# A message-passing layer on one core: the work after the last group of edges, in another order and another form

## The chip, the cores and the metric

The kernel runs on one core of one Trainium2 chip. The metric is device time in microseconds (us); the time before is the median of three runs, 1493.0 us (1492.52 to 1494.01). Durations of single instructions come from one separate execution that the hardware profiler recorded; that execution is longer as a whole (see the section on the profile).

## The reference

There are N = 6250 nodes with F = 64 features, and E = 200000 edges sorted by destination. For every edge a small network makes M = 9 weights, the source node's row is multiplied with them and with `W_tp`, and the messages are summed by destination node. The sums are scaled and shifted per node, added to `x` and normalised:

```python
w = silu(edge_attr @ W1 + b1) @ W2 + b2
h_src = features[src]
msg = einsum('ef,em,fmg->eg', h_src, edge_sh * w, W_tp)
agg = segment_sum(msg, dst, num_segments=N) / sqrt(16)
gamma, beta = split(silu(c_noise[:, None] @ Wn1 + bn1) @ Wn2 + bn2, 2, axis=-1)
x = layernorm(x + agg * (1 + gamma) + beta, axis=-1)
```

## The kernel before

**Tiles and groups.** The edges are cut into tiles of 128 and the tiles into 98 groups of 16 (`NBLK`, `KB`); group 97, the last, has only 11 tiles. The nodes are cut into 49 blocks of 128 (`NJ`). Since the edges are sorted, the edges of one tile end in at most W = 7 neighbouring nodes, and a group's edges in at most 256 nodes.

**What happens to a group.** Most of its source rows are gathered into `hs` by indirect DMAs that GpSimd issues six groups ahead. The last four tiles' rows (three in every fifth group) are instead picked from a copy of `x` in SBUF by matmuls: `pick(g, t)` (L488) multiplies one-hot matrices with `x` in 14 fp32r matmuls (L500) into the PSUM tile `px`, and VectorE reduces that to `hs` in two instructions (L509, L511). `hidden` (L429), `second` (L447) and `weights` (L457 to L467) make the edge weights, spread over the 7 windows, in `a`. `windows(g)` (L533) multiplies each tile's `hs` with its `a` into `pz`, and ScalarE copies `pz` into the SBUF tile `ztw` (L543), a slot for each of four groups. In the last group, tiles of even and odd number go to two PSUM tiles (the second is `pz__`).

**From windows to nodes.** `project(q)` multiplies the `ztw` of a pair of groups (2q-1 and 2q) with `W_tp` (L579), copies the result to SBUF (L582), turns it with a transpose (L585) and splits it into two fp32r halves, high and low, in `r` (L553 on ScalarE, L554 on VectorE). A group without a partner, as the last, is multiplied the other way round, without the transpose (L573). `marks(q)` (L563) makes the one-hot matrices `c` that say to which of 256 nodes a window belongs. `place(q)` (L595) multiplies `r` with `c`: features (high and low half) on partitions, 256 nodes on columns. The first 128 columns, added to the carried columns of the pair before, are `yt` of a finished block (L604); the other 128 are kept as `carry` (L601). `bring` (L612) multiplies `yt` with an identity and so puts the nodes on partitions and sums the two halves; `finish` runs the instructions of `finish_nodes` (L716 to L731), among them one square root on ScalarE (L728), and puts the store of the output (L382) on a list; SyncE issues it later.

**The order** is written out by hand: each engine gets its instructions in program order. In the loop each group's steps are put between the matmuls of the picks of the next group, so that TensorE always has pick matmuls to do. The end of the kernel, after the loop, is a list of calls. Before the change it is: `second(97)`, picks 1 and 2 of group 97, `windows(96)`, pick 3 of group 97 (the last pick), `project(48)`, which is the pair of groups 95 and 96, the three last tiles of `windows(97)`, transpose, halves and `place(48)`, `bring` of blocks 46 and 47 and most of their `finish`, the eight first tiles of `windows(97)`, the rest of that `finish`, `project(49)` (group 97 alone), `place(49)`, `bring` of block 48, its `finish`, and the stores. After them every engine reads a flag that decides on a general path (not taken here), and the program ends.

```python
            pick(g, 3)
            marks(g // 2)
            turn = project(g // 2)
            windows(g, [ZT])
            ends = []
            for f in turn + place(g // 2, psum.tile([P, 2 * P], F32, tag="s", name="ps_l")):
                f()
```

Of the kernel before, what the change touches and what calls it, by code (L numbers as in the profile page):

```python
# [7 lines left out]
F32 = mybir.dt.float32  # L8
# [59 lines left out]
def gnn_resnorm_kernel(ctx: ExitStack, tc: tile.TileContext, x, src, dst, dst_row, ea, sh, cn,  # L68
# [18 lines left out]
    with ExitStack() as fast:  # L87
# [354 lines left out]
        def second(g):  # L442

            s = st.pop(g)
            p2[g] = psum.tile([P, 2, 2 * P], F32, tag="s", name=f"p2_{g}")
            for c in range(KB // 4):
                nc.tensor.matmul(p2[g][c * D:(c + 1) * D, 0, :].rearrange("p (i e) -> p i e", i=2), w2p,  # L447
                                 s[:, :, c * P:(c + 1) * P], start=True, stop=True)
            p2s[g] = work.tile([P, 2 * P], F32, tag="p2s", name=f"p2s{g}")
            nc.scalar.activation(p2s[g], p2[g][:, 0, :], AF.Identity, bias=b2c)  # L450
# [37 lines left out]
        def pick(g, t, other=()):  # L488


            other = [f for fs in other for f in fs]
            q = picked(g) if g < NBLK else 0
            if t >= q:
                for f in other:
                    f()
                return
            px = psum.tile([P, F, J], F32, tag="px", name=f"px{g}_{t}", bufs=2)
            for h in range(J):
                for i in range(2):
                    nc.tensor.matmul(px.rearrange("p f l -> p (f l)"), hot_k[g, t][:, h, :],  # L500
                                     xs[i][:, h].rearrange("p f l -> p (f l)"),
                                     start=(h == 0 and i == 0), stop=(h == J - 1 and i == 1))
                    if i == 1 and other:
                        other.pop(0)()
            for f in other:
                f()
            xm = late.tile([P, F, J], F32, tag="xm", name=f"xm{g}_{t}")
            c = (g + 1) * Q - q + t
            nc.vector.scalar_tensor_tensor(xm, li[:, None, :].to_broadcast([P, F, J]), jl[:, c:c + 1], px,  # L509
                                           op0=ALU.is_equal, op1=ALU.mult)  # L510
            nc.vector.tensor_reduce(hs[g][:, tiles(g) - q + t, :], xm, AX.X, ALU.add)  # L511
# [7 lines left out]
        def windows(g, k0s=None):  # L519

            nk = tiles(g)
            end = g == NBLK - 1
            hsg, ag = hs[g], a[g]
            z = zs[g] if g in zs else sums(g)


            for k0 in range(0, nk, ZT) if k0s is None else k0s:
                n = min(ZT, nk - k0)
                pz = [psum.tile([P, ZT // 2, M, W], F32, tag="pz", name=f"pz{g}_{k0}", bufs=2)]
                pz.append(psum.tile([P, ZT // 2, M, W], F32, tag="px", name=f"pz{g}_{k0}_", bufs=2) if end else pz[0])  # L530
                for k in range(n):
                    v = k % 2
                    mm = nc.tensor.matmul(pz[v][v * F:(v + 1) * F, k // 2].rearrange("p m w -> p (m w)"),  # L533
                                          hsg[:, k0 + k, :], ag[:, k0 + k].rearrange("p m w -> p (m w)"),
                                          start=True, stop=True)
                    if k0 + k == 0:

                        for d in hs_dma.pop(g)[(g not in SPG):]:
                            tc.add_manual_dep(mm.ins, d.ins.name, mybir.DependencyInfo(
                                mybir.DependencyClass.Sync, mybir.DependencyReason.DATA), reason="rows of the group")  # L540
                for v in range(2):
                    for h in range(2):
                        nc.scalar.copy(  # L543
                            z[h * F:(h + 1) * F, 0:5 - h, k0 + v:k0 + n:2, :].rearrange("p m k w -> p k m w"),
                            pz[v][v * F:(v + 1) * F, 0:(n + 1 - v) // 2, h:M:2, :])

# [10 lines left out]
        def marks(q):  # L557

            for g in pair(q):
                if g in hot:  # L560
                    continue
                hot[g] = work.tile([KW, 2 * P], F32R, tag="c", name=f"c{g}")
                nc.vector.tensor_scalar(hot[g], nf[0:KW], nid[0:KW, g:g + 1], None, op0=ALU.is_equal)  # L563
# [26 lines left out]
        def place(q, pd):  # L590

            gs = pair(q)

            def part(k):
                nc.tensor.matmul(pd, r[q][:, k].rearrange("p s f -> p (s f)"), hot.pop(gs[k]),  # L595
                                 start=(k == 0), stop=(k == len(gs) - 1))
                if k == len(gs) - 1:
                    r.pop(q)
                    if q < NJ:
                        carry[q] = work.tile([P, P], F32, tag="carry", name=f"carry{q}")  # L600
                        nc.scalar.copy(carry[q], pd[:, P:2 * P])  # L601
                    if q > 0:
                        yt[q - 1] = work.tile([P, P], F32, tag="yt", name=f"yt{q}", bufs=3)
                        nc.vector.tensor_add(yt[q - 1], pd[:, 0:P], carry.pop(q - 1))  # L604

            return [lambda k=k: part(k) for k in range(len(gs))]

        def bring(j0, j1, py, ends=None):


            def part(j):
                nc.tensor.matmul(py[:, j - j0], yt.pop(j), ident2, start=True, stop=True)  # L612
                if j == j1 - 1:
                    finish(j0, j1, py[:, 0:j1 - j0], ends)

            return [lambda j=j: part(j) for j in range(j0, j1)]
# [21 lines left out]
        with tc.manual_schedule(), tc.tile_pool(name="temp", bufs=1) as temp:  # L638
            setup(temp)

            for i in range(NBLK):
                if i + AHEAD < NBLK:
                    gather(i + AHEAD)
                while stores:
                    stores.pop(0)()
                if i % LB == 0 and i + LB < NBLK:
                    if i > 0:
                        load(i + LB)
                    near(i + LB)
                if i % LB == 1 and i + 1 + LB < NBLK:  # L650
                    load_keys(i + 1 + LB)
                if i % 4 == 3 and i + 1 < NJ:
                    gate_load(i + 1)
                for g in SPG:
                    if AHEAD - SPS < g - i <= AHEAD:
                        load_rows(g, (AHEAD - g + i) * SPR)
                more = []
                if i + 2 < NBLK:
                    keys(i + 2)
                    more = [lambda: hots(i + 2, 0, 2)]  # L660
                pick(i + 1, 0, [nodes(i), more])
                if i + 2 < NBLK:
                    hots(i + 2, 2, Q)
                if 56 <= i <= 58:
                    reach(i - 56)
                if i + 2 < NBLK:
                    hidden(i + 2)
                if i == NBLK - 2:
                    break
                second(i + 1)  # L670
                windows(i)
                turn = project(i // 2) if i % 2 == 1 else []
                if i % 4 == 1 and i - 1 < NJ:
                    gate_hidden(i - 1)
                pick(i + 1, 1, [weights(i + 1), turn])
                for t in range(2, Q):
                    pick(i + 1, t)

            g = NBLK - 1
            second(g)  # L680
            nc.scalar.activation(root, eps, AF.Sqrt)
            pick(g, 1, [weights(g)])
            pick(g, 2)
            sums(g)
            windows(g - 1)
            pick(g, 3)
            marks(g // 2)
            turn = project(g // 2)
            windows(g, [ZT])
            ends = []  # L690
            for f in turn + place(g // 2, psum.tile([P, 2 * P], F32, tag="s", name="ps_l")):
                f()
            marks(NBLK // 2)
            for f in bring(NJ - 3, NJ - 1, psum.tile([P, FB, F], F32, tag="s", name="py_l"), ends):
                f()
            windows(g, [0])
            ends.pop()()
            project(NBLK // 2)
            ps = psum.tile([P, 2 * P], F32, tag="p1", name="ps_n")
            for f in place(NBLK // 2, ps) + bring(NJ - 1, NJ, psum.tile([P, 1, F], F32, tag="r", name="py_n")):  # L700
                f()
            while stores:
                stores.pop(0)()

# [205 lines left out]
```

## Time and profile before

| what | value |
|---|---|
| median of three runs | 1493.0 us |
| the profiled execution | 2388.12 us, of which the span from first to last instruction is 2386.3 us |
| granted TensorE clock, mean | 0.841 of full speed |
| TensorE matmul busy | 1675.3 us (70%) |
| VectorE, ScalarE, GpSimd busy | 1206.6, 521.1, 1109.7 us |
| pick matmuls (L500) | 5208, of 406 ns each on average |
| GpSimd idle before its gathers, waiting for L533 | 825.8 us |
| VectorE's last instruction (L731) | ends 2380.40 us after the span's start |

The profiled execution takes 1.6 times as long as an ordinary one, so the shares of the page describe a stretched body. Its end can be read by itself: it is a short stretch, every instruction of it has a start and a duration, and the pick matmuls there take 3.02 us for 14, about 0.21 us each. Each view below counts microseconds from the start of the span.

### The profile page before, as it was taken

How to read it: one execution, taken by the hardware profiler on the slowest of the kernel's cores; microseconds unless marked ns; L12 is line 12 of the kernel's file. 1: busy time of each engine (PE TensorE's matmuls, PEld its weight loads, DVE VectorE, ACT ScalarE, POOL GpSimd, SP SyncE). 2: the span in 40 equal slices, each digit the busy share in tenths (PEclk: the TensorE clock that was granted, in tenths of full speed). 3: DMA queues.
4: the chain of work that ended last, by engine and by line, in shares of the span. 5: the costliest groups of instructions: out<-in, count | busy, mean ns of one | idle time of the engine just before them, and what ended most of it. 6: DMA issues, size and time to landing. Idle time of an engine off the chain costs nothing. (4 is left out here: it accounts for less than half of the span.)

```text
span 2386.3 us, 34188 instructions
## 1 busy us (share of the span) xinstructions
PE 1675.3 (70%) x10858; PEld 1367.1 (57%) x10858; DVE 1206.6 (51%) x2157; ACT 521.1 (22%) x1326; POOL 1109.7 (47%) x1177
## 2 busy tenths in 40 slices
PE   3076777676776767677767677677777676877797
PEld 2065656564655655556656556565656564656586
DVE  3154545454545454545555545454545454545476
ACT  1021212121212121211222222121212121212133
POOL 7644444444444545444545454545444544444410
PEclk7598888888888988887888898788887888888898
DMA  3121111111111111111111111111111111111110
GB/s 114 34 62 40 47 34 41 36 46 37 38 35 42 41 39 38 44 37 38 35 36 44 38 37 45 35 36 35 47 34 37 36 45 35 37 35 46 33 38 5
DMA packets 90264, 96.13 MB, mean 40 GB/s; under 512 B 36744, under 2 KB 51290, under 8 KB 90074
## 3 DMA queue, kind: packets, MB, share of 16 engines
q1 hardware_dynamic: 52122, 53.89, 7.9%
q0 software_dynamic: 37376, 38.35, 7.1%
q8 instruction: 89, 1.46, 0.2%
q10 hardware_dynamic: 576, 1.61, 0.2%
q14 instruction: 101, 0.83, 0.1%
HBM read 92.01 MB, written 1.73 MB: 39 GB/s over the span
## 5 line engine op out<-in xcount | busy, mean ns | idle before, releaser
L99 POOL DMA_INDIRECT hs<-in_x_dram,src_i x1168 | 1108.4, 949 | 1167.6 <-PE pz L533 825.8
L500 PE MATMUL px<-xs_w,hot_k 128*128 128x448 f32 x5208 | 1304.3, 406 | 432.3 <-DVE xm L509 377.0
L500 PEld LDWEIGHTS px<-xs_w,hot_k 128*128 128x128 f32 x5208 | 1067.0, 213 | 567.4 <-DVE xm L509 409.5
L509 DVE SCALAR_TENSOR_TENSOR xm<-li,jl,px 128x448 f32<-128x448 f32 x372 | 251.8, 677 | 936.4 <-remote 698.0
L485 DVE TENSOR_TENSOR hot_k<-pk,nk 128x896 fp32r<-128x896 f32 x372 | 387.7, 1081 | 2.8 <-PE pk L233 2.8
L511 DVE TENSOR_REDUCE hs<-xm 128x64 f32<-128x448 f32 x372 | 230.6, 620 | 12.9
L438 ACT ACTIVATE st<-p,b1c 128x1024 f32<-128x1024 f32 x98 | 109.2, 1115 | 542.4 <-PE p L429 365.3
L543 ACT COPY ztw<-pz 64x140 f32<-64x140 f32 (+1 forms) x780 | 209.2, 268 | 21.7 <-PE pz L533 10.3
L447 PE MATMUL p<-st,w2p 128*32 128x256 f32 x784 | 71.8, 430 | 152.4 <-DVE xb L370 102.9
L601 ACT COPY carry<-ps 128x128 f32<-128x128 f32 x48 | 12.8, 266 | 649.4 <-PE ps L595 587.0
L533 PEld LDWEIGHTS pz<-a,hs 128*64 128x64 f32 x3116 | 116.5, 155 | 58.7 <-issue 55.1
L447 PEld LDWEIGHTS p<-st,w2p 128*32 128x32 f32 x784 | 17.6, 113 | 228.7 <-issue 127.1
L533 PE MATMUL pz<-a,hs 128*64 128x63 f32 x3116 | 131.7, 244 | 11.7 <-issue 11.5
L467 DVE TENSOR_TENSOR a<-oh,p 128x1008 f32<-128x1008 f32 x98 | 117.9, 1203 | 3.3
L429 PE MATMUL p<-ea,w1bd 64*128 64x512 f32 x392 | 111.5, 642 | 0.7 <-issue 0.7
L728 ACT ACTIVATE var<-var,eps 128x2 f32<-128x2 f32 (+1 forms) x25 | 7.4, 295 | 374.6 <-DVE var L725 374.6
L579 PE MATMUL pt<-ztw,wtc 128*64 128x112 f32 x960 | 71.9, 308 | 18.6 <-ACT st L438 18.6
L579 PEld LDWEIGHTS pt<-ztw,wtc 128*64 128x64 f32 x960 | 61.7, 170 | 20.6 <-ACT st L438 20.3
L554 DVE TENSOR_TENSOR r<-pt,r 112x128 fp32r<-112x128 f32 x48 | 13.9, 289 | 97.2 <-issue 86.2
L479 ACT CAST pk<-kr 128x512 f32<-128x512 f16 (+1 forms) x96 | 54.6, 569 | 16.5 <-DVE hot_k L485 11.1
L450 ACT ACTIVATE p2s<-p,b2c 128x256 f32<-128x256 f32 x98 | 45.9, 468 | 48.6 <-issue 30.5
L457 DVE STREAM_TRANSPOSE p<-p2s 128x256 f32<-128x256 f32 x98 | 44.1, 450 | 14.9 <-issue 14.4
(138 smaller groups left out, 552.7 us busy)
## 6 DMA issues: line engine op xcount, KB each, us to landing
hs<-in_x_dram SPq DMA_DIRECT2D x2944, 0.2 KB
ea<-in_ea_dram SPq DMA_DIRECT2D x48, 512.0 KB
hs<-in_x_dram,src_i POOLq DMA_INDIRECT x1168
kr<-kd SPq DMA_DIRECT2D x48, 256.0 KB
sh<-in_sh_dram SPq DMA_DIRECT2D x49, 144.0 KB
cb<-cn_d SPq DMA_DIRECT2D x12, 128.0 KB
out_dram<-o SPq DMA_DIRECT2D x24, 64.0 KB
dst_i<-in_dst_dram SPq DMA_DIRECT2D x1, 768.0 KB
```

Source lines behind the costliest of these rows:

```text
L99: hs_dma[g] = [nc.gpsimd.indirect_dma_start(out=hs[g][:, t - g * KB, :], out_offset=None, in_=x, in_offset=bass.IndirectOffsetOnAxis(ap=sr ...
L429: nc.tensor.matmul(p1[:, i, :].rearrange("p (c t e) -> p c t e", c=4, t=4), w1bd[i * 64:(i + 1) * 64, :], e[i * 64:(i + 1) * 64, :].rearra ...
L438: nc.scalar.activation(st[g], p1_t.pop(g), AF.Silu, bias=b1c)
L447: nc.tensor.matmul(p2[g][c * D:(c + 1) * D, 0, :].rearrange("p (i e) -> p i e", i=2), w2p, s[:, :, c * P:(c + 1) * P], start=True, stop=True)
L467: nc.vector.tensor_mul(a[g], oh_t.pop(g)[:, :, None, :].to_broadcast([P, KB, M, W]), sw.unsqueeze(3).to_broadcast([P, KB, M, W]))
L485: nc.vector.tensor_tensor(hot_k[g, t], pk_t[g][:, t, None, :].to_broadcast([P, J, P]), nk.unsqueeze(2).to_broadcast([P, J, P]), op=ALU.is_ ...
L500: nc.tensor.matmul(px.rearrange("p f l -> p (f l)"), hot_k[g, t][:, h, :], xs[i][:, h].rearrange("p f l -> p (f l)"), start=(h == 0 and i ...
L509: nc.vector.scalar_tensor_tensor(xm, li[:, None, :].to_broadcast([P, F, J]), jl[:, c:c + 1], px, op0=ALU.is_equal, op1=ALU.mult)
L511: nc.vector.tensor_reduce(hs[g][:, tiles(g) - q + t, :], xm, AX.X, ALU.add)
L533: mm = nc.tensor.matmul(pz[v][v * F:(v + 1) * F, k // 2].rearrange("p m w -> p (m w)"), hsg[:, k0 + k, :], ag[:, k0 + k].rearrange("p m w ...
L543: nc.scalar.copy(z[h * F:(h + 1) * F, 0:5 - h, k0 + v:k0 + n:2, :].rearrange("p m k w -> p k m w"), pz[v][v * F:(v + 1) * F, 0:(n + 1 - v) ...
L579: nc.tensor.matmul(pt[h * F:(h + 1) * F, 0, 0:KW], wtc2[:, c, :], z[h][:, c], start=(c == 0), stop=(c == 4))
```

## The change

The end of the kernel is rewritten; the loop before it stays. Block 46 is brought and finished by itself, between picks 1 and 2 of group 97, and stored early. `windows(96)` goes ahead of pick 2, and `project(48)` ahead of pick 3, its transpose and halves among the matmuls of pick 3. Blocks 47 and 48 are not placed as columns and turned: their sums are formed with the nodes on partitions from the start, in one PSUM tile `py_n`. Block 47 is the carried half times the identity plus four products of one-hot matrices with the halves in `r`; block 48 is four such products plus group 97's part. The eight first tiles of `windows(97)` go ahead of the three last, and of the copies to `ztw` of the three last tiles one PSUM tile's go to VectorE. The product of group 97 with `W_tp` is copied to SBUF by VectorE, unsplit, and added to block 48 by one fp32 matmul, whose one-hot matrix is read as fp32. The two blocks are finished and stored together.

```diff
@@ windows @@
                 for v in range(2):
+                    copy = nc.vector.tensor_copy if end and k0 == ZT and v == 1 else nc.scalar.copy
                     for h in range(2):
-                        nc.scalar.copy(
+                        copy(
                             z[h * F:(h + 1) * F, 0:5 - h, k0 + v:k0 + n:2, :].rearrange("p m k w -> p k m w"),
                             pz[v][v * F:(v + 1) * F, 0:(n + 1 - v) // 2, h:M:2, :])
@@ the end @@
             g = NBLK - 1
+            q = NJ - 1
             second(g)
             nc.scalar.activation(root, eps, AF.Sqrt)
             pick(g, 1, [weights(g)])
-            pick(g, 2)
+            ends = []
+            for f in bring(q - 2, q - 1, psum.tile([P, 1, F], F32, tag="r", name="py_l"), ends):
+                f()
+            windows(g - 1)
             sums(g)
-            windows(g - 1)
-            pick(g, 3)
-            marks(g // 2)
-            turn = project(g // 2)
+            pick(g, 2, [ends])
+            pick(g, 3, [project(q)])
+            while stores:
+                stores.pop(0)()
+            py = psum.tile([P, FB, F], F32, tag="s", name="py_n")
+            nc.tensor.matmul(py[:, 0], carry.pop(q - 1), ident2, start=True, stop=False)
+            for b in range(2):
+                for k, h in enumerate(pair(q)):
+                    for s in range(2):
+                        nc.tensor.matmul(py[:, b], hot[h][:, b * P:(b + 1) * P], r[q][:, k, s],
+                                         start=(b == 1 and k == 0 and s == 0), stop=(b == 0 and k == 1 and s == 1))
+            windows(g, [0])
+            marks(NJ)
             windows(g, [ZT])
-            ends = []
-            for f in turn + place(g // 2, psum.tile([P, 2 * P], F32, tag="s", name="ps_l")):
-                f()
-            marks(NBLK // 2)
-            for f in bring(NJ - 3, NJ - 1, psum.tile([P, FB, F], F32, tag="s", name="py_l"), ends):
-                f()
-            windows(g, [0])
-            ends.pop()()
-            project(NBLK // 2)
-            ps = psum.tile([P, 2 * P], F32, tag="p1", name="ps_n")
-            for f in place(NBLK // 2, ps) + bring(NJ - 1, NJ, psum.tile([P, 1, F], F32, tag="r", name="py_n")):
-                f()
+            z = zs.pop(g).rearrange("p c k w -> p c (k w)")
+            pr = psum.tile([P, F], F32, tag="r", name="pr_n")
+            for c in range(5):
+                nc.tensor.matmul(pr[0:KW], z[:, c], wtc2[:, c, :], start=(c == 0), stop=(c == 4))
+            last = work.tile([KW, F], F32, tag="rt", name="last")
+            nc.vector.tensor_copy(last, pr[0:KW])
+            nc.tensor.matmul(py[:, 1], hot[g][:, 0:P].bitcast(F32), last, start=False, stop=True)
+            finish(q - 1, NJ, py)
             while stores:
                 stores.pop(0)()
```

## The prediction, written before the changed kernel ran

> **What bounds the kernel now.** I read the granted clock first (one core, 0.841 on average over the span), then the chain of waits, since a change to the last few microseconds can only matter if those lie on it in full. They do. The chain of waits in order of time, columns start, duration and what ran, from the last picks on:
>
> ```profile
> 2315.60 0.96 PE pt L579 x20
> ...
> 2343.07 1.18 PE pt L579 x20
> ...
> 2362.45 1.08 PE pz L533 x32
> 2363.53 3.02 PE px L500 x14
> 2366.55 0.03 issue
> ...
> 2369.82 0.52 PE ps_l L595 x2
> ...
> 2371.01 0.66 PE py_l L612 x4
> ...
> 2373.49 2.14 PE pr L573 x10
> ...
> 2376.24 0.60 PE ps_n L595
> ...
> 2377.20 0.70 PE py_n L612 x2
> ...
> 2380.18 0.22 DVE o L731
> ```
>
> The last pick's matmuls end at 2366.55 (call it T). Up to there TensorE is never without work. From there each engine waits for another, and the last `o` is written at 2380.40, which is T + 13.85 us. That is the stretch that the change rewrites. The rows of L579 show that two groups take 27.5 us there (2315.60 to 2343.07), 13.7 us a group; 98 such groups are 1346 us, and the first product with `W_tp` in the timeline below comes at 147.75, so an ordinary run of 1493.0 must go about as fast as this end of the profiled one, and the profiled body (24 us a group) does not. I therefore take the end as it stands, and carry only the difference over: profiled time 2388.12 (span 2386.3 and 1.8 around it) less the gain, and 1493.0 less the same gain.
>
> Next I asked for the busy times and clock in short windows, because L573 looked slow. Columns: the stretch and its length, busy us and instructions of PE, PEld, DVE, ACT and POOL, then granted clock, DMA share, GB/s:
>
> ```profile
> 2371.00:2372.00 1.00, 0.99 (x17) 0.93 (x19) 0.51 (x2) 0.00 (x0) 0.00 (x0) 1.00 0.00 0
> 2372.00:2373.00 1.00, 0.31 (x10) 0.14 (x6) 0.87 (x4) 0.65 (x3) 0.00 (x0) 0.56 0.07 16
> 2373.00:2374.00 1.00, 0.51 (x3) 0.51 (x3) 0.75 (x3) 0.58 (x3) 0.00 (x0) 0.50 0.00 0
> ```
>
> A clock of 0.56 in the slice from 2372 means that full speed ended near 2372.1, T + 5.6, and everything TensorE does later runs at half. The timeline has the same L573 product at full clock in the setup, and the finish of two blocks:
>
> ```profile
> 147.75 1.17 PE L573 MATMUL pr<-wtc,ztw 128*112 128x64 f32 x10 [1.70 <-issue]
> 2371.59 0.13 PEld L533 LDWEIGHTS pz<-a,hs 128*64 128x64 f32 x1
> 2371.70 0.29 DVE L716 TENSOR_TENSOR y<-py_l,gam 128x128 f32<-128x128 f32 x1 [0.49 <-PE py_l L612]
> 2372.33 0.55 ACT L543 COPY ztw<-pz 64x140 f32<-64x140 f32 x2 [1.70 <-PE pz__24738 L533]
> 2380.43 0.35 SPq L382 DMA_DIRECT2D out_dram<-o  x1
> ```
>
> So 1.17 us at full clock, 2.14 at half: 0.97 us turn on when the clock falls.
>
> **What the Trainium skill says.** "TensorE: Matmul & The Clock Gate", Part 1, says that TensorE falls to half its clock after an idle window of about 3.4 us whose phase is free-running. The trace agrees in kind (1.00, then 0.50), and the phase makes the moment differ from run to run. The same page, section LDWEIGHTS, says that a weight load costs by its columns, not its rows, P / 1.2 ns; that is 107 ns for 128, and the setup's ten loads of 112 columns took 1.06 us, 106 ns each. The same page, Part 1 (architectural detail), calls ScalarE's and VectorE's queues strictly first in, first out; the trace's order agrees. "PSUM — Partial Sum Buffer", Specifications, says that ScalarE and VectorE may read PSUM side by side if they use different banks; the trace of before has no case in this step, as ScalarE makes all copies.
>
> **The change part by part.** First what moves ahead of the last pick, where TensorE is busy, so it is paid in full there. L579, 20 matmul passes: 0.96 us (row at 2315.60). The transpose L585: 0.11 us in the chain. `bring` of block 46 alone: two of the passes of L612, of which four took 0.66 with 0.27 of fill, so 0.13 a pass, 0.25 together. `windows(96)` only changes places with pick 2. The last pick now ends at T' = T + 1.32.
>
> What has to be hidden there: ScalarE's eight copies of group 96 end 2.97 us after its first `pz` load (2362.38 to 2365.35); the load stands 1.08 + 2.9 us ahead of L579, so they are ready with 1.0 us to spare. Block 46's finish puts seven VectorE instructions (0.22 us and a gap of 0.03 each, 1.7) behind pick 1's L511, then the memset, then a reciprocal that waits for ScalarE's square root, which waits behind those eight copies; pick 2's L509 stands behind it. By these rows `o` of block 46 is done about when pick 2's matmuls end. A slip of up to a microsecond delays pick 2's two instructions only: pick 3 has the other `px` tile, and TensorE waits for nothing of it. `r` and the two `c` (0.27, 0.29, 2 x 0.35) follow the transpose, which stands after six of the fourteen matmuls, so they end before T'. Its store is one DMA more on SyncE's queue, which waits there for nothing else. GpSimd's queue has ended its gathers.
>
> After T', with `py_n` (1 carried product in two passes and eight products of 64 columns, 128-column weights): ten passes. The trace has no fp32r product of 64 columns; the bounds are 0.106 (the setup's loads) and 0.145 a pass (four L612 passes before the next load, 2371.01 to 2371.59). I take 0.13, 1.3 us; as a successor starts 0.09 before its forerunner's end, the first `pz` load is at T' + 1.2. VectorE's L509 and L511 for the last pick (0.69 and 0.63) end at T' + 1.37, so they are hidden: only the three last tiles need them, and those now come second. From the first `pz` load to ScalarE's first copy 0.74 (2371.59 to 2372.33): T' + 1.95. ScalarE then makes six copies: four of eight tiles took 1.13 (2372.33 to 2373.46), two of `pz_8` 0.43, together 1.56; VectorE's two (I take 0.18 each, the ScalarE rows) run beside them, as does `marks(49)`, 0.35. L573 starts at T' + 3.55. At full clock it takes 1.17, to 4.72; VectorE's copy of 112x64 with its wait 0.04 + 0.22, to 4.98; the fp32 product 0.04 + 0.41 (two passes of L612), to 5.43; then the finish of two blocks, 2.97 with its wait (2371.70 to 2374.67), and 0.03 ahead of it: T' + 8.43, that is T + 9.75. Against 13.85 it gains 4.1 us with the clock held to the end. With the clock at half from L573 on, 0.97 and 0.29 more: it gains 2.85.
>
> The store has 64 KB in place of 32. Its data had moved 1.3 us after the issue for 64 KB and 1.2 for 32 (DMA share in windows of 0.2 us), while the span goes on 5.9 us after the issue; I put the difference between 0 and 0.2 and take 0.
>
> Where the clock falls is chance. Before, full clock ended 5.6 us after T with dense work until about T + 1; now dense work ends at T' and half-dense work (the ten passes and `windows(97)`) at about T' + 2.2, and L573 runs from 3.55 to 4.72. So a fall in the middle of L573 or just after is likeliest, half of the 1.26 us lost: a gain of 3.5.
>
> **The rivals.** (B) The clock falls before L573, as TensorE idles from T' + 2.2: a gain of 2.85, 1490.15. For it: before, the fall came after four idle-ish microseconds, and a free-running window can end early. Against: the full fall needs the window to end in about one microsecond of 3.4. (C) A wait takes the place of those removed: ScalarE's queue late for L579, or VectorE's chain (reciprocal, L509, `r`, `c`) late for the ten passes. The 1.0 us of slack would have to be overrun by 2; the gain is then about 1.5, 1491.5. Against: every row above fits. (D) The other side: products of 64 columns do not follow each other but each takes what a lone one took, 0.58 us (`ps_n` at half clock, nearest row). Eight of them cost 4.65 in place of 1.04, 3.6 more, and TensorE then counts as idle and stays at half clock, 1.26 against the full sum: 4.1 - 3.6 - 1.26 = -0.8, 1493.8. It decides from 0.49 us a product on (4.1 - 1.26 over eight, and the 0.13), with the clock at half. Against: L612's 64-column passes do follow each other at 0.145. That the instructions do not stand in the order described is excluded: the order of the instructions on each engine follows the calls.
>
> **How the numbers follow.** The forecast (A, clock held through some or all of L573) is 1493.0 - 3.5 = 1489.5, with 1488.7 to 1490.1 for it alone; chance 0.62. B 0.23, C 0.10, D 0.05. No measurement here tells less than 0.2%, 3.0 us, from no change, so faster means below 1490.0: nearly all of A, a third of B with the error of its sum. Slower counts only the upper part of D, from 0.9 us a product, and what I have not seen. That gives 0.67 faster, 0.29 within, 0.04 slower. The range 1488.4 to 1491.0 holds A, B and the low end of C, and takes in the bounds of the ten passes (0.24 us down, 0.15 up) and of the store; it leaves out most of C and D. The profiled execution as a whole cannot be held against this, its body varies by more; its end can: last `o` 9.75 to 11.0 us after where T was.
>
> **What would show it.** In the profile after: L579 inside the picks without a gap on TensorE; ten passes of `py_n` in 1.1 to 1.5 us after the last pick; ScalarE's first copy of group 97 about 1.95 us after it; L573's successor 1.2 us long (clock 1.00), 2.1 (0.50) or between; the last `o` about 8.4 to 9.7 us after the end of the last pick. I am wrong if TensorE idles ahead of the last pick, if a narrow product takes over 0.3 us, or if the end after the store grows.

## The result and the profile after

| | before | after |
|---|---|---|
| median of ten runs, us | 1492.78 (1491.98 to 1494.32) | 1488.91 (1488.53 to 1492.53) |
| ratio, 95% interval | | 0.9973 (0.9965 to 0.9981) |
| profiled execution: span, us | 2386.3 | 1486.9 |
| last edge-weight product of TensorE (L447) to the end of the span, us | 30.29 | 27.25 |
| end of the last pick (T, T') to the end of the last instruction (L731, L740), us | 13.85 | 9.05 |

The change makes the kernel 3.9 us faster; by the interval of the ratio it is between 2.8 and 5.2 us. In some executions the loop takes 24 us a group in place of about 14 (the profiled one of before, and every one of the first runs of split_copies, before_warm and all_three below, with medians of 2414, 2423 and 2427 us where before had 2423), so spans and medians of the two kinds are not comparable, and the ends are: the last two rows of the table.

The last row leaves out what was moved ahead of the last pick, so its difference of 4.80 us is not the gain. The row above it holds everything from the last L447 on; there the gain is 3.04 us.

This is the chain of waits of the kernel after, in order of time, from the end of pick 1 on; columns are start, duration, and what ran. The changed kernel has its own line numbers: L544, L580 and L586 are L543, L579 and L585 of before, L694 and L698 are the products of `py_n`, L706 is the product of group 97 with `W_tp` (L573 before), L709 the product that adds it to block 48, and L740 the last `o` (L731 before).

```profile
1463.29 0.17 PE py_l L612 x2
1463.46 1.08 PE pz L533 x32
1464.54 3.00 PE px L500 x14
1467.54 1.11 PE pt L580 x20
1468.65 1.41 PE px L500 x6
1470.06 0.11 PE pt L586
1470.17 1.61 PE px L500 x8
1471.78 0.17 PE py_n L694 x2
1471.95 0.87 PE py_n L698 x8
1472.82 0.20 PE pz L533
...
1473.48 0.26 ACT ztw L544
...
1475.06 1.78 PE pr_n L706 x10
...
1476.86 0.24 DVE last L708
...
1477.14 0.70 PE py_n L709 x2
...
1480.54 0.29 DVE o L740
```

The reader should see two things. Up to 1471.78, the end of the last pick, each row is TensorE and each starts where the one above ends: what was moved ahead is paid in full there and brings no idle time. After it the chain changes engine only five times (to ScalarE's copies, L706, VectorE's copy, L709 and the finish), where the chain of before went through the last pick's rows, three tiles, `r`, `ps_l`, `carry`, `yt` and `py_l` before its eight tiles, and through `r`, `ps_n`, `yt` and `py_n` after L573 (its lines are shown with the first experiment).

The clock, from the busy times in windows of 1 us of the kernel after (length, busy us of PE, PEld, DVE, ACT and POOL, granted clock, DMA share, GB/s):

```profile
1474.00:1475.00 1.00, 0.00 (x0) 0.00 (x0) 0.02 (x1) 0.95 (x5) 0.00 (x0) 1.00 0.00 0
1475.00:1476.00 1.00, 0.94 (x7) 0.94 (x8) 0.00 (x0) 0.00 (x1) 0.00 (x0) 0.74 0.00 0
1476.00:1477.00 1.00, 0.83 (x5) 0.64 (x4) 0.14 (x1) 0.00 (x0) 0.00 (x0) 0.50 0.00 0
```

A clock of 0.74 over the slice is 0.48 us at full and 0.52 at half speed: it fell at about 1475.5, inside L706, which therefore takes 1.78 us, between the 1.17 and the 2.14 of the prediction.

### The profile page after: what moved, and what is told of

Its sections match the earlier page's. It is cut to its first block, busy times and chain, and to the rows that moved or that the text cites. A ratio compares the mean times of both kernels' runs of the same rounds, so it can differ in the third digit from the quotient of the medians.

```text
span 1486.9 us, 34194 instructions
## 1 busy us (share of the span) xinstructions
PE 1440.4 (97%) x10863; PEld 1205.8 (81%) x10863; DVE 1202.6 (81%) x2157; ACT 514.2 (35%) x1322; POOL 1108.6 (75%) x1177
## 3 DMA queue, kind: packets, MB, share of 16 engines
HBM read 92.01 MB, written 1.73 MB: 63 GB/s over the span
## 4 chain that ended last, share of the span: by engine, by line
PE 81%; POOL 6%; DVE 6%; issue 3%; DMA 2%; ACT 2%; DVEq 0%; POOLq 0%
PE px L500 62%; PE pz L533 6%; POOL hs L99 6%; PE p L429 5%; PE pt L580 3%; PE p L447 3%; DMA hs<-in_x_dram,src_i 2%; ACT L438 1%; DVE xm L509 1%; PE ps L596 1%; ACT st L438 1%; DVE hs L511 1%; DVE hot_k L485 1%; PE ps L625 1%; DVE y L726 0%
## 5 line engine op out<-in xcount | busy, mean ns | idle before, releaser
L500 PE MATMUL px<-xs_w,hot_k 128*128 128x448 f32 x5208 | 1120.1, 370 | 2.1 <-ACT xs_w L247 1.3
L500 PEld LDWEIGHTS px<-xs_w,hot_k 128*128 128x128 f32 x5208 | 956.6, 189 | 81.1 <-DVE xs_w L248 3.3
L544 ACT COPY ztw<-pz 64x140 f32<-64x140 f32 (+1 forms) x780 | 208.6, 267 | 13.3 <-PE pz__24734 L533 3.0
L533 PEld LDWEIGHTS pz<-a,hs 128*64 128x64 f32 x3116 | 99.5, 138 | 43.1 <-issue 42.1
L533 PE MATMUL pz<-a,hs 128*64 128x63 f32 x3116 | 112.6, 225 | 3.0 <-issue 1.6
L447 PEld LDWEIGHTS p<-st,w2p 128*32 128x32 f32 x784 | 15.8, 108 | 86.3 <-issue 43.1
L447 PE MATMUL p<-st,w2p 128*32 128x256 f32 x784 | 62.7, 391 | 12.5 <-DVE xb L370 7.9
L580 PE MATMUL pt<-ztw,wtc 128*64 128x112 f32 x960 | 55.3, 261 | 3.0 <-ACT st L438 2.5
L429 PEld LDWEIGHTS p<-ea,w1bd 64*128 64x128 f32 x392 | 29.8, 186 | 29.2 <-issue 25.1
L461 DVE TENSOR_TENSOR p<-p,sh 128x72 f32<-128x72 f32 x196 | 47.3, 241 | 6.7
L580 PEld LDWEIGHTS pt<-ztw,wtc 128*64 128x64 f32 x960 | 46.8, 137 | 5.0 <-ACT st L438 3.9
```

The source lines that it names most:

```text
L429: nc.tensor.matmul(p1[:, i, :].rearrange("p (c t e) -> p c t e", c=4, t=4), w1bd[i * 64:(i + 1) * 64, :], e[i * 64:(i + 1) * 64, :].rearra ...
L544: copy(z[h * F:(h + 1) * F, 0:5 - h, k0 + v:k0 + n:2, :].rearrange("p m k w -> p k m w"), pz[v][v * F:(v + 1) * F, 0:(n + 1 - v) // 2, h:M ...
L580: nc.tensor.matmul(pt[h * F:(h + 1) * F, 0, 0:KW], wtc2[:, c, :], z[h][:, c], start=(c == 0), stop=(c == 4))
```

## The experiments

All times below are read against the kernel before, run on the same chip. Two figures come from each profile: "tail", from the start of the last L447 to the end of the span, and "path", from the end of the last pick to the end of the last `o`. Executions of one kernel differ by 2 to 3 us for reasons ahead of the end (see the last section), so where a median and a tail disagree by that much the tail is what I read. A tail is one execution; the spans are given to 0.1 us, and what follows the last `o` varies by 0.2 us. What each kernel is, is said in its paragraph below.

| kernel | path | tail | median | before, median | ratio (95% interval) |
|---|---|---|---|---|---|
| before, ordinary profile | 14.08 | 30.59 | 1496.02 | 1495.75 | 0.9998 (0.9989 to 1.0007) |
| after, again | 8.81 | 27.06 | 1491.42 | 1495.75 | 0.9969 (0.9956 to 0.9981) |
| late_project | 12.25 | 28.80 | 1492.14 | 1493.37 | 0.9989 (0.9983 to 0.9996) |
| only_ahead | 13.30 | 31.22 | 1493.35 | 1493.37 | 1.0002 (0.9994 to 1.0011) |
| act_copies | 9.57 | 27.61 | 1489.49 | 1493.37 | 0.9979 (0.9970 to 0.9988) |
| warm | 8.24 | 26.52 | 1489.30 | 1493.37 | 0.9970 (0.9960 to 0.9981) |
| before_warm, second | 12.62 | 29.37 | 1491.97 | 1493.49 | 0.9989 (0.9982 to 0.9995) |
| split_copies, second | 7.91 | 26.08 | 1489.13 | 1493.49 | 0.9966 (0.9953 to 0.9978) |
| all_three, second | 7.42 | 25.52 | 1488.75 | 1493.49 | 0.9967 (0.9955 to 0.9980) |

**Was the base of the sum right?** The prediction's sum was made on the profiled execution of 2388 us, so both kernels were profiled once more, unchanged, in executions of some 1490 us.

> The kernel before, unchanged, for a profile of an ordinary execution (1493 us) in place of one with a stretched loop (2388). My theory (the end of the stretched execution is the same stretch): from the last edge-weight product's start to the end of the span 30.3 us, up to 1.5 less where the clock falls later; from the last pick to the last instruction 13.9, up to 1.5 less. Rival (the end too was stretched there): 28 us or less, and the sum of the prediction was made against a wrong base.

> The changed kernel, unchanged, a second execution beside it on the same chip. My theory: from the last edge-weight product's start to the end of the span 27.3 us, between 26.3 (clock held to the end) and 27.6 (fallen before the last product with W_tp); the product 1.2 to 2.1 us by where the clock falls. Median 3 to 4 us below before.

The chain of waits of the kernel before in this execution:

```profile
1472.13 3.02 PE px L500 x14
...
1477.78 0.28 ACT r L553
...
1478.08 0.30 DVE r L554
...
1478.96 0.28 ACT carry L601
...
1479.26 0.30 DVE yt L604
...
1479.61 0.66 PE py_l L612 x4
...
1482.31 2.14 PE pr L573 x10
...
1484.53 0.22 ACT r L553
...
1484.77 0.24 DVE r L554
...
1485.67 0.30 DVE yt L604
...
1489.01 0.22 DVE o L731
```

The last pick ends at 1475.15; L573 again takes 2.14 us, and the path is 14.08 us against 13.85. The end was not stretched. The changed kernel's tail is 27.06, with L706 at 1.53 us because the clock fell 0.3 us later than in its first profile. By the tails the two pairs of profiles give 3.0 and 3.5 us of gain. The medians beside the second pair differ by 4.3 us (0.9969, which by its interval is 2.8 to 6.6 us), so they cannot decide whether the gain is nearer 3 or 4.

**The parts alone.** The change has a move (the product of groups 95 and 96 into the last pick) and a new form (the two last blocks summed with nodes on partitions, the last product unsplit). Each was made without the other; block 46's early finish and the eight tiles ahead of the three go with the new form here and are not told apart from it, and `windows(96)` ahead of pick 2 is in both. First the new form, with the move of the product undone:

```diff
-            pick(g, 3, [project(q)])
+            pick(g, 3)
+            for f in project(q):
+                f()
```

> The changed kernel with the product of groups 95 and 96 with W_tp put back behind the last pick. My theory (what counts is the serial path after the last pick): the last pick ends 1.2 us earlier, but the product (1.1), the copy to SBUF, the transpose, the two halves and the two one-hot matrices stand after it one behind the other, so the first product of the eight last tiles starts 3.6 us after the last pick in place of 1.0. Net 1.4 us later than the changed kernel: about 2.5 us faster than before, 1490.3. Rival (the time is TensorE's work, wherever it stands): as the changed kernel, within 0.3 us. Rival (the early product is where all the gain is): as before, 1492.8.

Its chain of waits behind the last pick:

```profile
1472.50 1.13 PE pt L580 x20
...
1473.65 0.26 ACT rt L583
...
1473.96 0.34 PE pt L586
...
1474.32 0.27 ACT r L554
...
1474.62 0.29 DVE r L555
1474.91 0.27 DVE c L564
...
1475.32 1.05 PE py_n L700 x8
1476.37 0.20 PE pz L533
```

All six steps stand one behind the other, and the eight tiles start 3.87 us after the last pick (3.6 expected) where the changed kernel starts them 1.04 after. Its tail is 1.55 us longer (1.4 expected); 0.37 of this is the clock, as L708, the product of group 97, takes 2.15 us in place of 1.78. The rival that only the amount of TensorE's work counts is out, as is the one that the move is the whole gain: the median is still below before, by 1.2 us (between 0.0004 and 0.0017 of the time), and the tail is below the two tails of before by 1.5 and 1.8. That is less than the 2.5 expected. Part of the shortfall lies in the expectation: it took 1.4 us off the 3.9 of the medians, and by the tails the whole change gains 3.0 to 3.5.

Then the move alone, in the kernel before:

```diff
             pick(g, 1, [weights(g)])
-            pick(g, 2)
-            sums(g)
             windows(g - 1)
-            pick(g, 3)
-            marks(g // 2)
-            turn = project(g // 2)
+            sums(g)
+            pick(g, 2)
+            pick(g, 3, [project(g // 2)])
             windows(g, [ZT])
             ends = []
-            for f in turn + place(g // 2, psum.tile([P, 2 * P], F32, tag="s", name="ps_l")):
+            for f in place(g // 2, psum.tile([P, 2 * P], F32, tag="s", name="ps_l")):
                 f()
```

> The kernel before with only the move: the windows of group 96 ahead of pick 2, the product with W_tp of groups 95 and 96 among the matmuls of the last pick. My theory: the last pick ends 1.2 us later; behind it the three last tiles still wait for the last pick's rows (1.4 us), then ScalarE's four copies of them stand ahead of the carried half, and that, yt, and the turning products stand ahead of the eight other tiles. These start about 3.7 us after the last pick in place of 5.0, and 1.2 was paid for it: a gain of 0.1 us, 0.5 at most, 1492.6. Rival (the move is the gain): 2 us or more faster, 1490.8 or below.

It gains nothing: ratio 1.0002, and its tail is 0.6 to 0.9 us longer than that of before. The chain shows what stands there:

```profile
1473.07 0.34 PE pz L533 x2
...
1474.08 0.18 ACT ztw L543
...
1474.28 0.27 ACT carry L601
...
1474.58 0.30 DVE yt L604
...
1474.93 0.87 PE py_l L612 x4
1475.80 0.30 PE pz L533
```

The placing products (L595) have all they need at 1471.19, when VectorE has made `c`, but stand behind the three last tiles on TensorE and start at 1473.33; `carry` stands behind those tiles' copies on ScalarE; and the tiles wait for the last pick's rows. The eight tiles start 4.14 us after the last pick (3.7 expected) in place of 5.12: the wait for the product has been replaced by that one, and 1.44 us was paid for it ahead of the last pick's end (11.98 us from the last L447 on, in place of 10.54). In this profile the clock also fell earlier, 3.6 us after the last pick: L612 took 0.87 us in place of 0.66, and the eight tiles 1.10 in place of 0.68 and 0.90, so most of the longer tail is the clock. So neither part gives what both give. Whether the move needs the new form itself, or only its order with the eight tiles ahead of the three, is not shown: the kernel before with its eight tiles first was not run.

**The copies.**

```diff
-                    copy = nc.vector.tensor_copy if end and k0 == ZT and v == 1 else nc.scalar.copy
+                    copy = nc.scalar.copy
```

> The changed kernel with all copies of the last group on ScalarE. My theory: VectorE's two small copies (0.40 us) ran beside ScalarE's six; behind them they cost 0.19 + 0.18, so the last product with W_tp starts 0.37 us later, and the end with it, plus what a clock that falls in this time adds (up to 0.2). Rival (the copies are not on the path, the clock or the first copies are): no change.

The product of group 97 with `W_tp` starts 3.67 us after the last pick in place of 3.28 (3.28 in both profiles of the changed kernel), 0.39 later where 0.37 was expected, and the path is 0.52 longer, as the product also takes 1.91 us in place of 1.78. The tail is 0.36 longer and the ratio moves by 0.0006, too little to tell there. The copies are on the path. The opposite edit gives VectorE all copies of the odd tiles:

```diff
-                    copy = nc.vector.tensor_copy if end and k0 == ZT and v == 1 else nc.scalar.copy
+                    copy = nc.vector.tensor_copy if end and v == 1 else nc.scalar.copy
...
-            windows(g, [0])
             marks(NJ)
+            windows(g, [0])
```

> The changed kernel with VectorE making all the copies of the odd tiles of the last group (four of eight), and the one-hot matrix of group 97 made ahead of them. My theory (behind the last pick the copies to SBUF are the path): ScalarE has four copies, 0.98 us in place of 1.56, VectorE 0.9 beside it, so the product of group 97 with W_tp starts 0.5 us earlier than in the changed kernel, and if the clock then falls later in it, up to 0.3 more. Median 0.5 to 0.8 below the changed kernel's. Rival (both engines' copies get in each other's way at PSUM or at the tile): the copies take longer each and nothing is gained.

> The kernel of split_copies again, for a median where the loop takes 15 us a group. From its profile, where the last instruction ended 7.8 us after the last pick with the clock held (9.05 in the changed kernel's, with a fall in the last product): my theory 0.5 to 1.2 us below the changed kernel's 1488.9, 1488.2. Rival (the copies get in each other's way): 1488.9 or more.

```profile
1476.67 0.31 DVE ztw L544
...
1476.99 0.28 DVE ztw L544
...
1477.29 0.20 DVE ztw L544
...
1477.49 0.20 DVE ztw L544
...
1477.83 1.18 PE pr_n L706 x10
```

In this chain of waits (the second run) VectorE's copies have taken the path from ScalarE's: 0.31 and 0.28 for what ScalarE does in 0.28 and 0.25. ScalarE's four copies beside them end 0.99 us after their start, where the same four take 0.97 in the changed kernel, so the two hardly hinder each other. L706 starts 2.88 us after the last pick, 0.40 earlier than in the changed kernel (0.5 expected). The path is 1.14 us shorter: 0.40 is this, and 0.75 is L706 at 1.18 in place of 1.78 and L709 at 0.55 in place of 0.70, as the clock fell only 4.6 us after the last pick. The first run's profile repeats the start (2.89) and has a path of 7.81, with both products at full clock (1.18 and 0.45). The medians do not show the 0.5 to 1.2 us expected: 0.9966 against 0.9973 and 0.9969 for the changed kernel.

**The clock.** Seven more products whose result nobody reads, in TensorE's wait for the copies:

```diff
+            idle = psum.tile([P, 512], F32, tag="p1", name="idle")
+            for i in range(7):
+                nc.tensor.matmul(idle[:, 0:448], hot_k[g, 3][:, i, :], xs[0][:, i].rearrange("p f l -> p (f l)"),
+                                 start=True, stop=True)
             z = zs.pop(g).rearrange("p c k w -> p c (k w)")
```

> The changed kernel with seven more products of 448 columns, whose result nobody reads, in the 1.6 us in which TensorE waits for ScalarE's copies of the last group. My theory (the clock falls since TensorE idles there, and its last products pay for it): the clock stays at 1.00 through the last product with W_tp, 1.17 us in place of 1.78, and the last product 0.41 in place of 0.70. The end comes 0.9 us earlier than in the changed kernel's profile, and 0.5 to 1.0 earlier in the median: 1488.2. Rival (the fall is set by the picks' end, not by the idle stretch): no change, or some 0.1 later if the added products end after the copies.

```profile
1474.99 1.60 PE idle L705 x7
1476.59 1.01 PE pr_n L710 x10
...
1477.90 0.45 PE py_n L713 x2
```

The chain shows L706's counterpart at 1.01 us and L709's at 0.45: the clock held, and in the windows of this run it falls only at about 1480.1, 7.0 us after the last pick, where nothing of TensorE is left. The tail is 0.73 us shorter, not 0.9, since the seven delay L710, which starts 3.48 us after the last pick in place of 3.28. One profile alone could be chance, as the moment of the fall varies; the four other profiles with added products below held the clock as long or nearly so (6.6 us or more), and none of the nine without them held it beyond 5.6. So the idle stretch makes the clock fall, and it costs the changed kernel under a microsecond; the medians (0.9970 against 0.9973 and 0.9969) do not show that much. The same in the kernel before, five products after the transpose and five behind the eight tiles of group 97:

```diff
+            idle = psum.tile([P, 512], F32, tag="r", name="idle")
+            for i in range(5):
+                nc.tensor.matmul(idle[:, 0:448], hot_k[g, 3][:, i, :], xs[0][:, i].rearrange("p f l -> p (f l)"),
+                                 start=True, stop=True)
```

> The kernel before with twice five more products of 448 columns, whose results nobody reads, in the two stretches in which TensorE waits: after the transpose of groups 95 and 96, and during the copies of group 97's eight first tiles. My theory (half clock costs the kernel before 1.0 us in L573, 0.3 in its last placing product and 0.3 in the last turning one): the clock stays at 1.00 and the end comes 1.5 us earlier than in the profile of before, so of the whole gain of the change some 0.5 us is clock and the rest is a shorter path. Rival (the clock is most of the gain): 3 us or more faster than before. Rival (the clock is nothing): as before.

> The kernel of before_warm again, for a median where the loop takes 15 us a group. From its profile, 12.6 us from the last pick to the last instruction in place of 13.85: my theory 1.2 us below before. Rival (the clock is held there in most executions anyway): no difference.

L573 takes 1.18 us, the path is 12.62 (12.59 in the first run's profile) in place of 13.85 and 14.08, and the median is 1.5 us (0.0011) below before, by the interval between 0.7 and 2.7 us. Three microseconds are out, and so is nothing. The changed kernel loses to the clock too, so its gain holds only the difference. With the clock held in both, the tails are 29.37 here and 26.52 in warm: the kernel is 2.9 us faster by the shorter path alone. Of the 3.0 and 3.5 us of the two pairs, 0.2 and 0.7 are then the clock.

**All together.** Split copies, four products in the wait, and the sums of block 47 normalised up to their variance while the last product runs, so that only block 48's seven instructions and a common square root, reciprocal and product are left at the end:

```diff
+            moments(0)
...
-            nc.vector.tensor_copy(last, pr[0:KW])
+            nc.scalar.copy(last, pr[0:KW])
             nc.tensor.matmul(py[:, 1], hot[g][:, 0:P].bitcast(F32), last, start=False, stop=True)
-            finish(q - 1, NJ, py)
+            moments(1)
+            nc.scalar.activation(var, var, AF.Sqrt, bias=eps, scale=1.0 / F)
+            nc.vector.reciprocal(var, var)
...
+            nc.vector.tensor_mul(o, y, var.unsqueeze(2).to_broadcast([P, 2, F]))
```

> The changed kernel with three more edits: the copies of the odd tiles on VectorE, four products that nobody reads in TensorE's wait, and the sums of block 47 normalised up to its variance during the last product with W_tp, so that the last finish has seven instructions for one block (1.7 us) and only the square root, reciprocal and product for both; the copy of that product goes to ScalarE. My theory: the product starts 2.7 us after the last pick in place of 3.3, takes 1.05 in place of 1.8, the last fp32 product 0.45 in place of 0.70, and the finish 2.5 in place of 3.0: the last instruction ends 7.1 us after the last pick in place of 9.05, the median 1.5 to 2 us below the changed kernel's, 1487. Rival (VectorE, which now has copies and the sums of block 47, becomes the bound): 0.5 us or less.

> The kernel of all_three again, for a median where the loop takes 15 us a group. From its profile, 7.4 us from the last pick to the last instruction: my theory 1.6 us below the changed kernel's 1488.9, 1487.3. Rival (the clock is held in the changed kernel in most executions anyway): 1.0 us below, 1487.9.

The path is 7.42 us (7.43 in the first run's profile) and the tail 25.52, the shortest of all, 1.73 below the changed kernel's (1.95 expected of the path; 1.63 came). The median is 4.7 us below before. Against the changed kernel the intervals overlap (0.9955 to 0.9980 and 0.9965 to 0.9981), so that it is faster than after is shown in the profiles and not by the medians; the two were not timed beside each other.

## Why the prediction was right

The mechanism held: work was moved to where it costs little more than its own time, and a chain over many engines became a short one. The total came closer than its terms, which missed in both directions, and that part is luck.

- **What moves ahead of the last pick** was put at 1.32 us. It took 0.17 + 1.11 + 0.11 = 1.39 by its own rows, and 1.59 in effect: from the last L447 to the end of the last pick 10.54 us passed before and 12.13 after, the same in both pairs of profiles. The other 0.20 lies in the matmuls of the picks, 9.03 us in four pieces in place of 8.82 in two. The prediction had no term for cutting them up. It also took L579 at 0.96 us from one of its two rows, where the other has 1.18.
- **What hides it** held: ScalarE's copies of group 96 end at 1466.35, and L580 starts at 1467.47, 1.1 us of slack where 1.0 was expected. The narrowest place was VectorE's queue at block 46's finish, and it was met as described:

```profile
1466.90 0.22 DVE L740 TENSOR_TENSOR o<-y,var 128x64 f32<-128x64 f32 x1
1467.15 14.08 SPq L382 DMA_DIRECT2D out_dram<-o  x2
1467.47 1.18 PE L580 MATMUL pt<-ztw,wtc 128*64 128x112 f32 x20
1467.58 0.68 DVE L509 SCALAR_TENSOR_TENSOR xm<-li,jl,px 128x448 f32<-128x448 f32 x1 [0.45 <-PE px L500]
```

  In this timeline `o` of block 46 ends at 1467.12 and VectorE then waits 0.45 us for pick 2's matmuls. So rival C did not come.
- **The ten passes** of `py_n` were put at 1.3 us, between 1.06 and 1.45. They took 0.17 + 0.87 = 1.04, 0.104 each: just under the lower bound, and under the 1.1 to 1.5 that it named as a sign. By the rule in the section LDWEIGHTS of the Trainium skill's "TensorE: Matmul & The Clock Gate", columns over 1.2, a load of 128 columns comes to 107 ns as an estimate, and the eight fp32r products, 0.109 us each, agree; that the loads set their pace is likely by this and was not tried. (The loads of 112 columns that the prediction set beside this figure come to 93 ns by the same rule, and took 106.) Rival D, 0.58 us a product, is excluded: eight took 0.87.
- **From the last pick to L706**: 3.28 us where 3.55 was summed, ScalarE's first copy at 1.70 in place of 1.95. 0.25 of the difference is the term of the ten passes.
- **The clock** fell inside L706, as taken for the likeliest, in both profiles (1.78 and 1.53 us). Rival B, a fall before it, came in neither. It cost 0.90 us in the first profile (0.61 in L706, 0.29 in L709) and 0.65 in the second, where half of 1.26, 0.63, was taken.
- **The finish and the store**: the finish took 2.96 us, 0.03 after L709. From the last `o` to the end of the span it is 6.07 us (6.12 in the second profile), before 5.90 and 5.97: some 0.15 for twice the bytes, inside the 0 to 0.2 and not the 0 that was taken. An end after the store that grows was one of the prediction's signs of being wrong; it came, with this size.
- **The sum**: path 9.05, between the 8.43 and 9.7 of the prediction. The first pair gives 13.85 - 1.59 - 9.05 - 0.17 = 3.04 us, the second 14.08 - 1.59 - 8.81 - 0.15 = 3.53. The forecast of 3.5 lies between these and the 3.9 of the medians: 0.27 too little for what was moved and 0.15 for the store stand against 0.27 too much up to L706, and the clock decides the rest. What the prediction did not have is how much two executions differ ahead of the end, which is why the medians can't be held against it to a microsecond.
- **The base** was right, as before_again shows, but the argument for it was right by luck. It added 98 groups of 13.7 us to a first product at 147.75 us and came to 1494. In before_again that product comes at 69.1 us, and from there to the last L447 it is 1395.5 us, 14.4 a group: a setup taken 79 us too long makes up for a loop taken 50 us too short and for the 30 us after it, which the sum left out. The two rows of L579 that it read are one pair of groups, 27.5 us apart; in before_again the next pair after such a one takes 29.8 (L579 at 1363.71, 1391.18 and 1421.02). Nor is TensorE quite "never without work" up to the last pick: it waits 0.23 us ahead of the L579 at 2343.07.

## What to carry to other kernels

At the end of a kernel, where engines wait for each other, count the changes of engine on the path and ask of each product whether a form exists that needs no copy between; an edit there can be worth nothing alone and 1.5 us beside another, as the early product was, since alone it only uncovers the next wait. Look also at who stands ahead in an in-order queue: here products that were ready, and the copy behind them, stood after tiles that waited for the last rows. And where TensorE idles ahead of its last products, read the granted clock in windows of a microsecond before a duration from elsewhere in the trace is used for them.

## What the runs showed of the hardware

**The moment of the fall is loose.** Full clock ended 5.6 and 5.3 us after the last pick in the two profiles of before, 3.7 and 4.0 in those of after, 4.0 in act_copies, 3.6 in only_ahead, 4.8 in late_project, 5.3 and 4.6 in the two of split_copies. With added products it ended at 7.0 us in warm, 7.7 and 6.6 in all_three, and 12.3 and 12.2 in before_warm. The Trainium skill ("TensorE: Matmul & The Clock Gate", Part 1) gives an idle window of about 3.4 us of free-running phase; that no fall came before 3.6 us fits it, but the runs don't show which busy share ends a window. Seven products of 0.23 us each were enough to hold it until TensorE had no more work, and in all_three four of 0.25.

**The spread of the medians comes from far ahead of the change.** The first product of a single group with W_tp stands at the end of the setup, the last L447 near the end of the loop. In the ten profiles of both kernels and their variants that have spans of 1485 to 1495 us the first comes at 66.9 to 69.5 us. Windows of the kernel after, then of before in its second profile, from 40 to 60 us:

```profile
40.00:60.00 20.00, 18.69 (x108) 15.08 (x108) 14.79 (x31) 6.30 (x18) 15.42 (x16) 0.78 0.66 145
```

```profile
40.00:60.00 20.00, 17.84 (x100) 13.56 (x101) 15.27 (x35) 6.58 (x19) 15.26 (x16) 0.74 0.61 130
```

The first reaches that product at 67.1 us, the second at 69.1, with TensorE less busy (17.84 us in place of 18.69) and at a lower clock. In all ten profiles, to within 0.01, a later first product goes with a lower clock in this stretch, from 0.80 at 66.9 us to 0.74 at 69.5. Which of the two makes the other is not shown, and nothing was tried.

From there to the last L447 seven of the ten take 1392.2 to 1392.7 us, and three 1395.1 to 1395.6. These three have waits of TensorE ahead of L533, the windows of a group, that the seven do not have: 2.0 us at 1449 in before_again, 1.43 and 1.84 at 1376 and 1450 in after_again, 1.58 and 1.43 at 1376 and 1449 in the second split_copies. What they wait for stays open. Each of the two differences, of 2 to 3 us, is nearly as large as the effect under study, lies ahead of the changed end, and is no part of it.
